# Cross-attention on one core: operand addresses, the first table load, a query copy and the bias load

## The chip, the core and the metric

The kernel runs on one core of a Trainium2 chip. The core has a matrix engine (TensorE, PE in the profile, with its weight loads shown apart as PEld), VectorE (DVE), ScalarE (ACT), GpSimd (POOL) and SyncE (SP). Each has its own instruction queue and works through it in order; they wait for each other through semaphores. DMA transfers are issued from the queues of SP, ACT or POOL. The metric is the device time of one execution in microseconds; lower is better. Operands lie in SBUF, 128 partitions wide; where this text gives the address of a tile, it is the byte offset inside a partition, and it is the allocator's, the same in every execution.

## The reference

Thirty-two batches of queries attend to 77 context rows each. Three of the four attention branches of the reference get an empty slice of the context (it has just the 77 text rows), so they add nothing, and what is left is

```python
# x: (32, 512, 640)   ctx: (32, 77, 1024)   20 heads of 32
q = heads(x @ to_q_w)
k, v = heads(ctx @ to_k_w), heads(ctx @ to_v_w)
p = softmax(q @ k.T / sqrt(32))
out = merge(p @ v) @ to_out_w + to_out_b + x
```

All of it is float32.

## The kernel before

A float32 product is made of three passes over halves: every large operand is split into a high part and a remainder (`split`, L88: a ScalarE copy that rounds, then a VectorE or GpSimd subtraction), and PE adds high·high, high·low and low·high into one PSUM bank (`PAIRS`, L117). Those matmuls have 128x128 weights and 512 streamed columns. Scores and the product with the values are left in plain float32; the trace shows two PE records for each of those.

The order of work is written by hand; no scheduler changes it. It has four stretches.

*Context* (0 to 251 us). Keys and values of all 2464 context rows are computed in five groups (four of 512 rows and one of 416). `load_context` (L139) and `load_weights` (L92) issue the loads; `first` (L271) takes the first group chunk by chunk while the weights still arrive: for chunk k it splits the context (`ct`), the key weights (`wk_s`) and the value weights (`wv_s`), does 15 key matmuls (`pk`) and 9 value matmuls (`pv`). Ahead of it 16 matmuls on a tile of zeros (L269) keep PE busy. In later groups 120 key and 120 value matmuls stand in a row. Results go through DRAM (`k_dram`, `v_dram`). Queues: SP issues most loads, ACT issues two quarters of the first key-weight chunk, POOL issues the first value weights after a small instruction that waits for the first context piece (`pause`, L297).

*Slots* (264 us to the end). There are 160 slots, n = 5b + j for batch b and head group j of four heads (`slot`, L649). Slot n does on PE the scores of n (`sc`, L458, weights `qt`, moving `kb`), the first nine matmuls of an output projection of an earlier batch (`po`, L571, weights `wo_s`, moving `at`), the 15 matmuls of the queries of n+1 (`pq`, L436, weights `wq_s`, moving `xt` or `xu`), the last six of `po`, and in every second slot the values of two earlier slots (`pa`, L518, weights `vb`, moving `raw`). The other engines do the row maxima (`nm`, DVE), the exponentials (ACT, L480), the division by the row sums (`pn`, POOL, L492), the transpose of the probabilities (`z`, DVE, L499), the move of `z` into `raw` (`move_p`, SP, L504), the copy of the queries out of PSUM (`qt`, `copy_q`, L444), splits of `x`, and bias and residual (POOL).

*The fill* is slots 0 to 8, while the pipeline has not got its full distance. There `copy_q` is on VectorE, and `transpose_p(n - 1)` stands ahead of it in a slot, apart from slots that `copied` names (L654: 3 and 4), in which copy comes first and transpose and `move_p` follow. In slot 6 `load_bias` (L411) issues five DMAs on SP: `bias` (one row broadcast to 128 partitions) and four quarters of `bias_y`. The semaphores of SP's DMAs go round in a ring of eight, so an issue waits until the DMA eight issues earlier has landed. The first reader of `bias_y` is `bias_of` (L550) in slot 9; `bias` is read in the last stretch.

*The end* (`end`, L746) finishes the last batch.

Addresses of the matmul operands modulo 512 bytes, before. Slices that a matmul takes of `wk_s`, `wv_s`, `wq_s`, `wo_s`, `ct`, `xt`, `xu`, `at` and `raw` start at multiples of 512 bytes inside their tiles, so each row holds for all matmuls of its kind:

| matmuls | weights | moving |
|---|---|---|
| `pk` | `wk_s` 352 | `ct` 480 |
| `pv` | `wv_s` 480 | `ct` 480 |
| `pq` (most) | `wq_s` 128 | `xt` 128 |
| `pq` (45 of 2400, slots 4 to 8) | `wq_s` 128 | `xu` 64 |
| `po` | `wo_s` 64 | `at` 64 |
| `sc` | `qt` 192 | `kb0` 128 + 308 j, `kb1` 160 + 308 j |
| `pa` | `vb` 192 + 128 i | `raw` 64 |

Of the kernel before, what the change touches and what calls it, by code (L numbers as in the profile page):

```python
# [8 lines left out]
F32 = mybir.dt.float32  # L9
FPR = mybir.dt.float32r  # L10
AF = mybir.ActivationFunctionType
ALU = mybir.AluOpType
# [11 lines left out]
P = 128  # L24
Q = 32
# [3 lines left out]
HPC = 4  # L29
# [8 lines left out]
def kernel(  # L38
# [25 lines left out]
    nc = tc.nc  # L64
    B, S, C = x.shape
    CA = ehs.shape[2]
    NT = B * NKEY
    NQ = S // P
    NC_ = C // P
    NK = CA // P  # L70
    HALF = C // 2
    G = 512
# [19 lines left out]
    def load_weights(w, k0, kn, permuted=True, queues=(nc.sync,) * 4, tag="wraw"):  # L92


        raw = kvw.tile([P, 2, C], F32, tag=tag, name="wraw", bufs=3 if tag == "wraw" else 2)
        if permuted:
            rows = w.rearrange("(q c i) n -> q i c n", q=4, i=Q)
            for q, queue in enumerate(queues):
                queue.dma_start(raw[q * Q : (q + 1) * Q, :kn], rows[q, :, k0 : k0 + kn])
        else:  # L100
            rows = w.rearrange("(c p) n -> p c n", p=P)
            nc.sync.dma_start(raw[:, :kn], rows[:, k0 : k0 + kn])
        for k in range(kn):
            wraws[id(w), k0 + k] = raw[:, k]

    def split_weights(dst, w, k, scale=None, turned=False):

        part = wraws.pop((id(w), k))
        if scale is not None:
            nc.scalar.mul(part, part, scale)  # L110
        hi, lo = dst[:, 0, :], dst[:, 1, :]
        if turned:
            part = part.rearrange("p (q c i) -> p c q i", q=4, i=Q)
            hi, lo = (d.rearrange("p (c q i) -> p c q i", q=4, i=Q) for d in (hi, lo))
        split(hi, lo, part)
# [23 lines left out]
    def load_context(g, *counts):  # L139

        g0, gn = GROUPS_KV[g]
        src = ehs_flat[g0 : g0 + gn, :].rearrange("(a j) (q u) -> q j a u", j=Q, q=4)
        if g not in css:
            css[g] = kvc.tile([P, G // Q, NK * Q], F32, tag="cs", name="cs"), [0]
        cs, done = css[g]
        for kn in counts:
            cols = slice(done[0] * Q, (done[0] + kn) * Q)
            for q in range(4):
                nc.sync.dma_start(  # L149
                    cs[q * Q : (q + 1) * Q, : gn // Q, cols], src[q, :, :, cols]  # L150
                )
            done[0] += kn
# [37 lines left out]
    def keys(g, j, k, *passes):  # L190
        w = wk_s[:, :, :, j * P : (j + 1) * P]
        context_product(pks, "pk", g, j, k, w, psk, *passes)
# [69 lines left out]
    ctx.enter_context(tc.manual_schedule(engines=ENGINES))  # L262


    zero = kvt.tile([P, G], FPR, name="zero")
    nc.vector.memset(zero.bitcast(F32), 0.0)
    warm = psk.tile([P, G], F32, tag="ps", name="warm")
    for _ in range(16):
        nc.tensor.matmul(warm, zero[:, :P], zero, start=True, stop=True)  # L269

    def first(*ks):  # L271

        for k in ks:
            transpose_context(0, k)
        for k in ks:
            if k == 0:
                split_weights(wk_s[:, k], wk, k)
            split_context(0, k)
            if k == 0:
                for n in (0, 2, 1):  # L280
                    for j in range(NC_):
                        keys(0, j, k, (n,))
            else:
                split_weights(wk_s[:, k], wk, k)
                for j in range(NC_):
                    keys(0, j, k)
            part = wraws.pop((id(wv), k))
            for (c0, c1), dst in zip(WV, wv_s):
                split(dst[:, k, 0], dst[:, k, 1], part[:, c0:c1])
            for j in range(3):  # L290
                values_of_chunk(0, j, k, psk)

    load_context(0, 1)
    load_weights(wk, 0, 1, queues=(nc.scalar, nc.scalar, nc.sync, nc.sync))
    pause = kvt.tile([Q, Q], F32, name="pause", bufs=1)
    probe = css[0][0][:Q, 0, :Q]
    nc.gpsimd.tensor_tensor(pause, probe, probe, ALU.add)  # L297
    load_weights(wv, 0, 1, queues=(nc.gpsimd,) * 4, tag="ws")
    load_context(0, 1)
    load_weights(wk, 1, 1)  # L300
# [95 lines left out]
    raws, ats, sms, pqs, pas, xrs, pos, scs, nms = ({} for _ in range(9))  # L396


    kbs = [main.tile([P, NC_, NKEY], F32, name=f"kb{n}") for n in range(2)]
    vbs = [main.tile([KPAD, NC_, HPC, HD], F32, name=f"vb{n}") for n in range(2)]  # L400
    pnb = []
# [9 lines left out]
    def load_bias():  # L411
        biases.append(late[0].tile([P, C], F32, name="bias"))
        biases.append(late[0].tile([P, U], F32, name="bias_y"))
        nc.sync.dma_start(biases[0], bo.unsqueeze(0).to_broadcast([P, C]))
        for q in range(4):
            nc.sync.dma_start(
                biases[1][q * Q : (q + 1) * Q, :],
                bo[q * U : (q + 1) * U].unsqueeze(0).to_broadcast([Q, U]),
            )
# [229 lines left out]
    def slot(n, beside=()):  # L649
# [1 line left out]
        ahead, more = n + 1 < N, b + 1 < B  # L651
        og, oc = b - GROUP[j][0], GROUP[j][1]
        filling = n < NC_ + 2
        copied = n in (3, 4)  # L654
        xsplits = (SPLIT_X if b else {0: (2,), 1: (3,), 2: (4,)}).get(j, ()) if more else ()
        turns = TRANSPOSE_X.get(j, ()) if more and b > 1 else ()
        taken = takes.get(n, ())
# [74 lines left out]
                low_a(m)  # L732
        if n in EARLY_X:
            split_x(2, EARLY_X[n])
        if n == NC_ + 1:
            load_bias()
        for c in xsplits if n != PAIRED - 1 else ():
            split_x(b + 1, c)
# [120 lines left out]
```

## Time and profile before

| | us |
|---|---|
| timed runs | 1737.1, 1742.2, 1742.19 (median 1742.19) |
| profiled execution, its own time | 1736.4 |
| span of its trace, first to last instruction | 1734.4 |
| PE busy | 1724.8 (99%) |
| ACT busy | 1129.3 |
| POOL busy | 985.5 |
| DVE busy | 975.0 |

The granted TensorE clock is 1.000 over the span. Busy time of PE is modelled at the ends of matmuls, which are pipelined; how fast it really goes is read from the distance between starts, or from the chain of work that ended last, in which a piece of PE runs from the end of one matmul to the end of the next. A line of that chain gives start, duration, what, and how many instructions were merged.

### The profile page before, as it was taken

To read this page: it belongs to the slowest core of one execution; us is meant where nothing else is said; L and a number is where in the kernel's file an instruction comes from. 1 tells how busy PE (TensorE), PEld (TensorE's weight loads), DVE (VectorE), ACT (ScalarE), POOL (GpSimd) and SP (SyncE) were. 2 spreads that over 40 slices of the span, in tenths; PEclk is the share of its full clock that TensorE was granted. 3 is DMA by queue.
4 is the path that set the end of the run, shared out by engine and by line. 5 is a ranking of instruction groups with operands and counts; after the bars stand their busy time and mean duration, and the time that the engine had idled before them with its cause. 6 is when DMAs were issued, how large, how long until landed. Compare 5 with 4: busy or idle time off the path is not lost.

```text
span 1734.4 us, 36819 instructions
## 1 busy us (share of the span) xinstructions
PE 1724.8 (99%) x12461; PEld 1312.0 (76%) x12461; DVE 975.0 (56%) x1559; ACT 1129.3 (65%) x5697; POOL 985.5 (57%) x658
## 2 busy tenths in 40 slices
PE   9999999999999999999999999999999999999999
PEld 7888898677777777777777777777777777777777
DVE  5342225756666566665665656556666566665653
ACT  3131126877777777777777777777777777777771
POOL 1000026666666666666666666666666666666665
PEclk9999999999999999999999999999999999999999
DMA  9846566978888888898988888888979798888875
GB/s 186 161 85 177 124 123 145 230 158 195 177 194 174 190 175 191 187 193 176 196 186 179 192 179 184 178 187 183 194 175 200 162 203 173 190 178 190 174 169 158
DMA packets 363979, 306.50 MB, mean 177 GB/s; under 512 B 88784, under 2 KB 292176, under 8 KB 363792
## 3 DMA queue, kind: packets, MB, share of 16 engines
q1 hardware_dynamic: 361200, 297.02, 79.3%
q0 software_dynamic: 2496, 6.97, 1.4%
q8 instruction: 99, 1.62, 0.4%
q14 instruction: 88, 0.72, 0.1%
q10 hardware_dynamic: 96, 0.16, 0.0%
HBM read 120.36 MB, written 57.88 MB: 103 GB/s over the span
## 4 chain that ended last, share of the span: by engine, by line
PE 98%; DMA 1%; SPq 0%; DVE 0%; issue 0%; ACT 0%; POOL 0%; DVEq 0%; ACTq 0%; POOLq 0%
PE po L571 32%; PE pq L436 31%; PE sc L458 10%; PE pa L518 8%; PE pk L182 8%; PE pv L182 8%; PE po L603 1%; DMA raw<-z 0%; DMA bias<-in_L_xattn_to_out_b_dram 0%; SPq L508 0%; DMA wraw<-in_L_xattn_to_k_w_dram 0%; POOL pn L492 0%; SPq L149 0%; DVE z L499 0%; DVE qt L445 0%
## 5 line engine op out<-in xcount | busy, mean ns | idle before, releaser
L480 ACT ACTIVATE pn<-sc,nm 128x77 f32<-128x77 f32 x2560 | 789.2, 364 | 228.8 <-DVE nm L470 191.8
L492 POOL TENSOR_TENSOR pn<-pn,rs 128x1232 f32<-128x1232 f32 x160 | 363.7, 2273 | 483.1 <-DVE rs L490 479.3
L480 ACT ACTIVATION_READ_ACCUMULATOR pn<-sc,nm 128x1 f32 x2560 | 623.3, 244 | 0.0
L571 PE MATMUL po<-at,wo_s 128*128 128x512 f32 x2325 | 601.0, 399 | 0.0
L436 PE MATMUL pq<-xt,wq_s 128*128 128x512 f32 x2355 | 564.9, 391 | 0.0
L436 PEld LDWEIGHTS pq<-xt,wq_s 128*128 128x128 f32 x2355 | 441.5, 188 | 97.2
L571 PEld LDWEIGHTS po<-at,wo_s 128*128 128x128 f32 x2325 | 424.5, 188 | 99.4 <-issue 0.8
L470 DVE TENSOR_REDUCE nm<-sc 128x4 f32<-128x308 f32 x640 | 261.4, 471 | 69.4 <-PE sc L458 69.3
L499 DVE STREAM_TRANSPOSE z<-pn 128x1536 f32<-128x1536 f32 x160 | 283.0, 1769 | 1.0 <-POOL pn L492 0.9
L458 PEld LDWEIGHTS sc<-kb,qt 32*128 32x128 f32 x5120 | 157.3, 186 | 97.6 <-ACT at L532 62.9
L259 POOL TENSOR_TENSOR xt<-xs,xt 128x512 fp32r<-128x512 f32 x157 | 198.1, 1287 | 36.0 <-ACT xt L258 36.0
L581 DVE STREAM_TRANSPOSE ot<-po 128x512 f32<-128x512 f32 x155 | 111.1, 717 | 189.2 <-PE po L571 189.2
L585 POOL TENSOR_TENSOR xs<-xs,ot 128x512 f32<-128x512 f32 x155 | 200.1, 1291 | 2.4 <-DVE ot L581 2.3
L552 POOL TENSOR_TENSOR xs<-xs,bias_y 128x640 f32<-128x640 f32 x124 | 193.5, 1572 | 7.3
L458 PE MATMUL sc<-kb,qt 32*128 32x77 f32 x5120 | 180.9, 277 | 1.9 <-DVE qt L445 1.8
L532 ACT CAST at<-pa 128x512 fp32r<-128x512 f32 x160 | 94.4, 590 | 134.7 <-PE pa L518 134.7
L490 DVE RECIPROCAL rs<-sm 128x16 f32<-128x16 f32 x160 | 40.4, 253 | 223.2 <-ACT pn L480 223.1
L518 PE MATMUL pa<-raw,vb 96*32 96x512 f32 x1280 | 154.9, 599 | 1.4 <-DMA raw<-z 1.4
L537 DVE TENSOR_TENSOR at<-pa,at 128x512 fp32r<-128x512 f32 x160 | 109.8, 686 | 79.1 <-ACT at L532 79.1
L182 PE MATMUL pk<-ct,wk_s 128*128 128x512 f32 (+1 forms) x600 | 136.1, 386 | 1.3 <-ACT ct L89 1.3
L182 PE MATMUL pv<-ct,wv_s 128*128 128x512 f32 (+1 forms) x600 | 134.1, 382 | 0.0
L182 PEld LDWEIGHTS pk<-ct,wk_s 128*128 128x128 f32 x600 | 112.8, 188 | 22.8 <-ACT ct L89 1.7
(41 smaller groups left out, 693.6 us busy)
## 6 DMA issues: line engine op xcount, KB each, us to landing
raw<-z SPq DMA_DIRECT2D x640, 192.0 KB, 4.4
xs<-in_x_dram SPq DMA_DIRECT2D x256, 320.0 KB, 6.4
out_dram<-xs SPq DMA_DIRECT2D x127, 320.0 KB, 5.1
vb<-v_dram SPq DMA_DIRECT2D x32, 240.0 KB, 5.6
kb<-k_dram SPq DMA_DIRECT2D x32, 192.5 KB, 6.2
cs<-in_ctx_dram SPq DMA_DIRECT2D x12, 512.0 KB, 9.1
k_dram<-ks POOLq DMA_DIRECT2D x20, 256.0 KB, 2.4
v_dram<-vs SPq DMA_DIRECT2D x80, 64.0 KB, 2.2
```

Source lines behind the costliest of these rows:

```text
L182: nc.tensor.matmul(held[j][:, :gn], w[:, k, a, :], cts[g, k][:, c, :gn], start=(k == 0 and n == 0), stop=(k == NK - 1 and n == 2),)
L259: low.tensor_tensor(parts[1], src, parts[0].bitcast(F32), ALU.subtract)
L436: nc.tensor.matmul(pqs[n], wq_s[:, k, a, j * P : (j + 1) * P], xts[b, k][:, c, :], start=(k == 0 and m == 0), stop=(k == NC_ - 1 and m == 2),)
L458: nc.tensor.matmul(sc[:, t, :NKEY], qt[r, t * P : (t + 1) * P], kbs[b % 2][r, j, :], start=True, stop=True, tile_position=(i * HD, 0),)
L470: nc.vector.tensor_reduce(nms[n][:, i], sc[:, :, :NKEY], AX.X, ALU.max, negate=True)
L480: nc.scalar.activation(pnb[n % 2][:, at, :NKEY], sc[:, t, :NKEY], AF.Exp, bias=nms[n][:, i, t : t + 1], accum_out=sms[n][:, at : at + 1],)
L492: nc.gpsimd.tensor_tensor(pf, pf, rs.unsqueeze(2).to_broadcast([P, NQ * HPC, NKEY]), ALU.mult)
L499: nc.vector.transpose(z.rearrange("p c h t j -> p (h t) c j"), pn.rearrange("p a (c i) -> p a c i", i=Q),)
L518: nc.tensor.matmul(pas[n][i * HD : (i + 1) * HD, :].rearrange("p (a q) -> p a q", q=P), vb[:, i, :], raw[:, :, i, :], start=True, stop=Tru ...
L552: nc.gpsimd.tensor_tensor(part, part, biases[1].unsqueeze(1).to_broadcast([P, 4, U]), ALU.add)
L571: nc.tensor.matmul(pos[b, c], wos[0][:, k, a, c * P : (c + 1) * P], ats[b * NC_ + k][:, d, :], start=(k == 0 and m == 0), stop=(k == NC_ - ...
L585: nc.gpsimd.tensor_tensor(part, part, ots.pop((b, c)).rearrange("p (a i) -> p a i", i=Q), ALU.add)
```

## The change

Five edits go together.

1. Addresses. `zero` gets one buffer instead of two; `pause` grows from 128 to 512 bytes; a tile `early` of 512 bytes is new; a tile `align` of 64 bytes, which nothing uses, is put at the front of the pool `main`. So `wk_s` moves to 480 modulo 512 (with `ct` and `wv_s` where they were), and everything in `main` and behind it moves up by 64 bytes: `xu`, `at`, `wo_s` and `raw` to 128, `qt` to 256, `kb0` to 192 + 308 j, `kb1` to 224 + 308 j, `vb` to 256 + 128 i. `wq_s`, `xt`, `ct` and `wv_s` stay. `pk` then has 480 and 480, and all `pq` and `po` have 128 and 128; for `sc` and `pa` the distance between the two operands stays as it was.
2. ScalarE copies 32 columns of `zero` into `early` ahead of its two DMA issues, and its first table load stands ahead of that copy. Before, the table load stood behind the two issues and the wait for the key weights.
3. In `first`, the context is split ahead of the key weights in every chunk (in chunk 0 it was the other way round), and the passes of chunk 0 go 0, 1, 2 and not 0, 2, 1. There are 15 matmuls on zeros and not 16.
4. Slot 5 is added to the slots in which `copy_q` stands ahead of `transpose_p` and `move_p`.
5. `load_bias` moves from slot 6 on SP's queue to slot 3 on GpSimd's.

```diff
--- before.py
+++ after.py
@@ -262,10 +262,10 @@
     ctx.enter_context(tc.manual_schedule(engines=ENGINES))
 
 
-    zero = kvt.tile([P, G], FPR, name="zero")
+    zero = kvt.tile([P, G], FPR, name="zero", bufs=1)
     nc.vector.memset(zero.bitcast(F32), 0.0)
     warm = psk.tile([P, G], F32, tag="ps", name="warm")
-    for _ in range(16):
+    for _ in range(15):
         nc.tensor.matmul(warm, zero[:, :P], zero, start=True, stop=True)
 
     def first(*ks):
@@ -273,28 +273,24 @@
         for k in ks:
             transpose_context(0, k)
         for k in ks:
-            if k == 0:
-                split_weights(wk_s[:, k], wk, k)
             split_context(0, k)
-            if k == 0:
-                for n in (0, 2, 1):
-                    for j in range(NC_):
-                        keys(0, j, k, (n,))
-            else:
-                split_weights(wk_s[:, k], wk, k)
+            split_weights(wk_s[:, k], wk, k)
+            for passes in ((0,), (1,), (2,)) if k == 0 else ((0, 1, 2),):
                 for j in range(NC_):
-                    keys(0, j, k)
+                    keys(0, j, k, passes)
             part = wraws.pop((id(wv), k))
             for (c0, c1), dst in zip(WV, wv_s):
                 split(dst[:, k, 0], dst[:, k, 1], part[:, c0:c1])
             for j in range(3):
                 values_of_chunk(0, j, k, psk)
 
+    early = kvt.tile([P, P], F32, name="early", bufs=1)
     load_context(0, 1)
+    nc.scalar.copy(early[:, :Q], zero[:, :Q].bitcast(F32))
     load_weights(wk, 0, 1, queues=(nc.scalar, nc.scalar, nc.sync, nc.sync))
-    pause = kvt.tile([Q, Q], F32, name="pause", bufs=1)
+    pause = kvt.tile([P, P], F32, name="pause", bufs=1)
     probe = css[0][0][:Q, 0, :Q]
-    nc.gpsimd.tensor_tensor(pause, probe, probe, ALU.add)
+    nc.gpsimd.tensor_tensor(pause[:Q, :Q], probe, probe, ALU.add)
     load_weights(wv, 0, 1, queues=(nc.gpsimd,) * 4, tag="ws")
     load_context(0, 1)
     load_weights(wk, 1, 1)
@@ -396,6 +392,7 @@
     raws, ats, sms, pqs, pas, xrs, pos, scs, nms = ({} for _ in range(9))
 
 
+    main.tile([P, HPC * NQ], F32, name="align")
     kbs = [main.tile([P, NC_, NKEY], F32, name=f"kb{n}") for n in range(2)]
     vbs = [main.tile([KPAD, NC_, HPC, HD], F32, name=f"vb{n}") for n in range(2)]
     pnb = []
@@ -411,9 +408,9 @@
     def load_bias():
         biases.append(late[0].tile([P, C], F32, name="bias"))
         biases.append(late[0].tile([P, U], F32, name="bias_y"))
-        nc.sync.dma_start(biases[0], bo.unsqueeze(0).to_broadcast([P, C]))
+        nc.gpsimd.dma_start(biases[0], bo.unsqueeze(0).to_broadcast([P, C]))
         for q in range(4):
-            nc.sync.dma_start(
+            nc.gpsimd.dma_start(
                 biases[1][q * Q : (q + 1) * Q, :],
                 bo[q * U : (q + 1) * U].unsqueeze(0).to_broadcast([Q, U]),
             )
@@ -651,7 +648,7 @@
         ahead, more = n + 1 < N, b + 1 < B
         og, oc = b - GROUP[j][0], GROUP[j][1]
         filling = n < NC_ + 2
-        copied = n in (3, 4)
+        copied = n in (3, 4, 5)
         xsplits = (SPLIT_X if b else {0: (2,), 1: (3,), 2: (4,)}).get(j, ()) if more else ()
         turns = TRANSPOSE_X.get(j, ()) if more and b > 1 else ()
         taken = takes.get(n, ())
@@ -732,7 +729,7 @@
                 low_a(m)
         if n in EARLY_X:
             split_x(2, EARLY_X[n])
-        if n == NC_ + 1:
+        if n == 3:
             load_bias()
         for c in xsplits if n != PAIRED - 1 else ():
             split_x(b + 1, c)
```

## The prediction, on record before the result

> **What bounds the kernel now.** I read the page first (busy time and chain), then the chain in order of time, then the records of single tiles, then the timeline of the start and of the fill.
>
> ```profile
> span 1734.4 us, 36819 instructions
> PE 1724.8 (99%) x12461; PEld 1312.0 (76%) x12461; DVE 975.0 (56%) x1559; ACT 1129.3 (65%) x5697; POOL 985.5 (57%) x658
> ...
> PE po L571 32%; PE pq L436 31%; PE sc L458 10%; PE pa L518 8%; PE pk L182 8%; PE pv L182 8%; PE po L603 1%; DMA raw<-z 0%; DMA bias<-in_L_xattn_to_out_b_dram 0%; SPq L508 0%; DMA wraw<-in_L_xattn_to_k_w_dram 0%; POOL pn L492 0%; SPq L149 0%; DVE z L499 0%; DVE qt L445 0%
> ```
>
> PE is the bound from end to end, and the set of matmuls doesn't change (but for one on zeros). So time can come from two places only: the few microseconds in which PE waits (start, fill), and the rate at which its matmuls follow each other. The rate isn't the same everywhere. The chain in order of time, context stretch:
>
> ```profile
> 64.24 27.89 PE pk L182 x120
> 92.12 27.21 PE pv L182 x120
> ...
> 174.42 27.89 PE pk L182 x120
> ...
> 229.52 22.42 PE pk L182 x120
> ...
> 255.35 9.04 PE pv L182 x48
> ```
>
> Same shapes, same moving tiles, one behind the other: 120 key matmuls take 27.89, that is 232.4 ns each, 120 value matmuls 27.21, or 226.8. What differs is the place of the weights: 352 against 480 modulo 512, with the moving operand at 480. In the last group, with 416 columns, keys take 187 ns and values 188: no difference there. The records of the two moving tiles of the queries say the same:
>
> ```profile
> L436 PE MATMUL pq<-xt,wq_s x2355: 387/389/506, 251.8 to 1690.4; 128*128 128x512 f32 x197
> ...
> L436 PE MATMUL pq<-xu,wq_s x45: 390/394/398, 301.0 to 329.2; 128*128 128x512 f32 x45
> ```
>
> With both at 128 the median is 389 ns, with `xu` at 64 it is 394. Equal is faster, by about 5 ns a matmul. In the slots all operands of `po` and nearly all of `pq` are already equal within a matmul, but the two kinds stand at different places (64 and 128). Two slots of the chain, and then the 15 `pq` matmuls of the second slot cut into the first ten and the last five:
>
> ```profile
> 905.33 2.30 PE po L571 x9
> 907.62 3.41 PE pq L436 x15
> 911.04 1.37 PE po L571 x6
> ...
> 915.33 2.24 PE po L571 x9
> 917.56 3.44 PE pq L436 x15
> ```
> ```profile
> 917.56 2.31 PE pq L436 x10
> ```
> ```profile
> 919.87 1.13 PE pq L436 x5
> ```
> ```profile
> 917.18 3.40 PEld L436 LDWEIGHTS pq<-xt,wq_s 128*128 128x128 f32 x15
> ```
>
> Behind the switch from `po`, ten matmuls take 231 ns each and then five take 226, the rate of the value matmuls. The first weights of `pq` are loaded from 917.18, while the last `po` matmul is still in the chain (to 917.56): one pair with operands at 64 and 128. I read this as a phase between the weight load and the stream that such a pair disturbs and that takes up to ten matmuls to come back.
>
> **The change, part by part**, against the profiled execution (1736.4, of which the span is 1734.4; two timed runs are at 1742.2, one at 1737.1, so it lies at the lower of two levels 5 us apart).
>
> *Addresses, keys.* Groups 1 to 3 have 120 key matmuls each of 512 columns: 3 x (27.89 - 27.21) = -2.0. Nothing hides it or takes it away, as the chain runs on PE from 64 to 252 us. Group 4 gains nothing. Group 0 is in the start, below. Ends: 0 and -2.7, the latter if group 4 gained in proportion.
>
> *Addresses, slots.* After the change `po` and `pq` all stand at 128, so a settled phase should live through both switches. 15 matmuls at 226.8 ns are 3.40. Slots come in two kinds that alternate: 3.44 becomes 3.40 (-0.04) and 3.41 becomes 3.40 (-0.01). The six `po` after `pq` take 1.37, at 226.8 they would take 1.36: -0.01 in both. That is -0.07 a pair; slots 8 to 159 are 76 pairs: **-5.3**. The nine `po` behind the scores also start unsettled (2.30 and 2.24; nine at the settled rate are 2.04), but there `wo_s`, `qt`, `kb`, `vb` and `raw` all move by the same 64 bytes, so I leave that cost. Better end: the 2.30 also becomes 2.24, -0.13 a pair, -9.9. Worse end: the phase never settles, and all of it runs at the 231 ns of those ten; that is the third rival, +12.9.
>
> *Addresses, `xu`.* 45 x 5 ns = -0.2, in the fill, where other waits take it up: 0.
>
> *The start.* Chain and timelines of the first microseconds:
>
> ```profile
> 3.31 2.76 DMA wraw<-in_L_xattn_to_k_w_dram
> ...
> 6.16 1.28 ACT L89
> ...
> 7.45 0.72 ACT wk_s L89
> 8.18 0.53 ACT ct L89
> ...
> 8.75 3.77 PE pk L182 x15
> ...
> 20.16 3.49 PE pk L182 x15
> ```
> ```profile
> 0.74 0.93 ACTq L99 DMA_DIRECT2D wraw<-in_L_xattn_to_k_w_dram  x2
> ```
> ```profile
> 4.88 0.71 DVE L157 STREAM_TRANSPOSE craw<-cs 128x512 f32<-128x512 f32 x1 [3.47 <-DMA cs<-in_ctx_dram]
> ...
> 19.28 0.83 DVE L90 TENSOR_TENSOR wk_s<-wraw,wk_s 128x640 fp32r<-128x640 f32 x1 [1.39 <-ACT wk_s L89]
> ```
> ```profile
> 1.46 6.00 PE L269 MATMUL warm<-zero 128*128 128x512 f32 x16 [1.46 <-DVE zero L266]
> ```
> ```profile
> DMA  0079879999999999999999999999999999999920
> ```
>
> The key weights land at 6.07; then table load 1.28, weight copy 0.72 and context copy 0.53 stand in a row, and PE begins at 8.75. After: the table load runs from 0.74 to 2.0 under the transfers, `early` takes some 0.2 by its 32 columns, and the two ACT issues follow to 3.15, ahead of SP's last one at 3.31, whose landing ended the wait and should still end it. The context (ready at 4.88 + 0.71 = 5.59) is copied while the weights land, weights 6.1 to 6.9; PE, with one matmul on zeros (6.00/16 = 0.38) less, is free at 7.1. So the first key matmul comes 1.6 earlier. That doesn't last: the DMA engines are busy from 2 to 34 us (last row, 40 slices of 0 to 35 us), and the remainder of chunk 2's weights is ready at 19.28 + 0.83 = 20.11, where its first user, the third matmul of `pk`, starts at 20.16 + 2 x 0.23 = 20.6. Only 0.5 can be kept; against it stand two quarters issued 1.5 later to a full DMA queue. I take -0.4. Better end -0.9 (all loads land a bit earlier), worse +0.4 (the 160 KB delayed are 0.8 us of the DMA, and half of it is not made up). The new order of copies and passes is hidden by the same loads. From chunk 5 on the loads are ahead and keys run at the new rate, 15 x 5.6 ns x 3 chunks = -0.3.
>
> *The fill.* Waits, chain, and timelines of VectorE and GpSimd:
>
> ```profile
> PE pa L518 <- DMA raw<-z: 1.4, 2, 0.9
> ```
> ```profile
> 310.78 1.13 PE sc L458 x32
> ...
> 319.52 7.87 DMA bias<-in_L_xattn_to_out_b_dram
> ...
> 328.67 4.07 DMA raw<-z
> ...
> 332.87 1.07 PE pa L518 x8
> ```
> ```profile
> 308.28 1.78 DVE L499 STREAM_TRANSPOSE z<-pn 128x1536 f32<-128x1536 f32 x1 [0.38 <-POOL pn L492]
> 309.99 0.65 DVE L445 COPY qt<-pq 128x512 f32<-128x512 f32 x1
> 311.48 0.25 DVE L490 RECIPROCAL rs<-sm 128x16 f32<-128x16 f32 x1 [0.84 <-ACT pn L480]
> ```
> ```profile
> 300.23 2.28 POOL L492 TENSOR_TENSOR pn<-pn,rs 128x1232 f32<-128x1232 f32 x1 [2.32 <-DVE rs L490]
> 305.97 2.28 POOL L492 TENSOR_TENSOR pn<-pn,rs 128x1232 f32<-128x1232 f32 x1 [3.46 <-DVE rs L490]
> ```
> ```profile
> L204 POOL DMA_DIRECT2D k_dram<-ks x20 | 10.9, 544 | 188.9 <-ACT ks L202 188.3 <-issue 0.2
> ```
>
> Bias: its first DMA takes 7.87 to land, SP's ring makes the issue of slot 7's `raw` wait for it (chain, 319.52 to 328.67), and PE stands 0.9 for that `raw`. Without the five issues on SP that `raw` lands some 3 us before its use: -0.85, and next in line is nothing that the chain shows. On GpSimd five issues at 544 ns are 2.7, in the gap of 3.46 between two divisions (302.5 to 305.97): hidden by 0.7; without that cover the division, the transpose behind it and the scores come later by what is over, +1 at the most by an issue at 0.9 each.
>
> The copy: in slot 5 it moves ahead of a transpose of 1.78 and can start as the queries end (about 309.0), so the scores of slot 6 come some 0.8 earlier. But slot 7's copy hangs on the division of slot 5, whose reciprocal (311.48) waits for ACT's exponentials, and those don't move. So most comes back as a wait of slot 7; the maxima of slot 6, now behind the transpose, win 0.25, and that I take. Together **-1.1**; ends -1.9 and +0.5.
>
> Sum: -2.0 - 5.3 - 0.4 - 0.3 - 1.1 = -9.1; 1736.4 - 9.1 = 1727.3 for an execution like the profiled one. On the two levels of the timed runs it is 1728.0 and 1733.1. The median of the new runs may be on either; I give the middle, 1731.
>
> [...]
>
> **The rivals.**
> First, keys gain and the switches don't: what settles in ten matmuls is the change of PSUM bank or of tile and not the 64 bytes. For it: both come at the same switch. Against it: `pv` changes its bank every 24 matmuls inside 27.21 and keeps 226.8 in the mean. 1736.4 - 2.0 - 0.4 - 0.3 - 1.1 = 1732.6 (1738.4 on the upper level), a gain of 0.2%.
> Second, addresses do nothing: keys are slow because of something else in their stretch. Then -0.4 and -1.1 remain: 1734.9, or 1740.7. Against it: `xu` shows the same 5 ns in another stretch.
> Third, slower: the phase of the slots rests on where `po` stands to the scores, and with all at 128 it doesn't settle. Place: every `po` and `pq` in slots 8 to 159. Price: `pq` at 231 ns, 2 x 15 x 0.231 = 6.93 against 6.85; the six `po` 1.39 against 1.37, twice; the nine `po` 2.30 against 2.24 in every second slot: +0.17 to a pair, x 76 = +12.9. With the rest 1736.4 + 12.9 - 3.8 = 1745.5, or 1751.3. It decides from about +0.12 a pair on, where the time passes 0.3% above before. For it: the start behind the scores is 2.30 in one kind of slot and 2.24 in the other with the same addresses modulo 512, so modulo 512 isn't the whole of it. Against it: `pq` at 128 and 128 does settle.
>
> **How the numbers follow.** My forecast has 0.66, the first rival 0.14, the second 0.07, the third 0.09; 0.04 is for more than forecast (the better end of the slots, 1722.7). The time is that of the forecast. 0.3% is about what a measurement here can tell from no change, 5.2 us: below 1737.0 is faster, above 1747.4 slower. The forecast gains 9.1 with bounds that leave it within 0.3% one time in ten, the first two rivals are within it, the third is above. Faster 0.64, same 0.27, slower 0.09. The range 1723 to 1739 runs from the better end of the forecast to the first rival on the upper level, and leaves out the third and part of the second.
>
> **What would show it.** In the chain after: `pk` x120 at 27.2; `pq` x15 at 3.40 in both kinds of slot and `po` x6 at 1.36; the `xu` median at 389; PE's first `pk` at about 7.1 but chunk 2's only some 0.4 earlier; no bias in the chain and no wait for `raw` in slot 8; a wait of PE ahead of slot 7's scores in place of slot 6's; five GpSimd issues between two divisions without shifting the second. Wrong it would be if `pq` still shows 3.44, or if the nine `po` take more than 2.30.

## The result, and the profile after

The changed kernel takes 1731.56 us (median of six executions, 1730.28 to 1735.23). The kernel before took 1741.14 (six executions with the three of its own page among them, 1737.1 to 1743.99). The ratio is 0.9958, with a 95% interval of 0.9945 to 0.9972. (Ratios here and below are taken over the executions that can be compared and are not the quotients of the two medians.) So it is faster by 0.28 to 0.55%, and the median lies half a microsecond from the forecast. Its terms came out less evenly, and one has the wrong sign.

The profiled execution took 1730.84. The first lines of its page, then its chain in order of time (start, length, engine, what), from the context stretch to slot 9:

```profile
span 1728.6 us, 36822 instructions
...
PE 1720.0 (100%) x12460; PEld 1313.9 (76%) x12460; DVE 974.6 (56%) x1559; ACT 1129.0 (65%) x5698; POOL 987.1 (57%) x663
```

```profile
63.49 27.20 PE pk L182 x120
90.69 27.20 PE pv L182 x120
...
226.69 22.40 PE pk L182 x120
249.09 3.43 PE pq L433 x15
...
335.07 2.29 PE po L568 x9
```

The key matmuls now take what the value matmuls take: 27.20 for 120, where they took 27.89. Two slots from the steady part of the same chain:

```profile
913.09 2.24 PE po L568 x9
915.33 3.40 PE pq L433 x15
918.73 1.36 PE po L568 x6
...
921.15 2.29 PE po L568 x9
923.44 3.41 PE pq L433 x15
926.85 1.36 PE po L568 x6
```

In the kind of slot whose nine `po` take 2.24, `pq` went from 3.44 to 3.40. In the other kind it stays at 3.41, and the six `po` are at 1.36 in both. The two moving tiles of the queries, by tile:

```profile
L433 PE MATMUL pq<-xt,wq_s x2355: 388/389/794, 248.9 to 1685.0; 128*128 128x512 f32 x197
...
L433 PE MATMUL pq<-xu,wq_s x45: 388/389/628, 298.1 to 329.7; 128*128 128x512 f32 x45
```

`xu` now has the median of `xt`, 389 where it had 394. The maxima, 794 and 628 ns where they were 506 and 398, belong to what went wrong.

The two spans differ by 5.8 us, and the chains say where. One more row of the kernel before, the nine `po` of slot 9:

```profile
335.00 2.27 PE po L571 x9
```

| stretch | before | after | difference | forecast |
|---|---|---|---|---|
| to the first key matmul of group 1 | 64.24 | 63.49 | -0.75 | -0.7 |
| groups 1 to 3, to the start of group 4 | 165.28 | 163.20 | -2.08 | -2.0 |
| group 4, to the first `pq` | 22.42 | 22.40 | -0.02 | 0 |
| fill, to the nine `po` of slot 9 | 83.06 | 85.98 | **+2.92** | **-1.1** |
| from there to the end | 1399.4 | 1393.5 | -5.9 | -5.3 |

Each start is read from a chain row and subtracted from the next one. Everything but the fill came out within 0.6. The fill lost 2.9 where a gain of 1.1 was expected. By stretches of 12 us, the fill of the kernel before and then of the kernel after (columns: stretch, its length, the busy time of PE, weight load, VectorE, ScalarE, GpSimd, then granted clock, DMA share and GB/s):

```profile
299.00:311.00 12.00, 11.24 (x110) 7.46 (x103) 10.11 (x17) 11.65 (x71) 5.82 (x3) 1.00 0.75 193
311.00:323.00 12.00, 11.66 (x119) 7.85 (x118) 9.68 (x16) 11.27 (x68) 5.81 (x3) 1.00 1.09 257
323.00:335.00 12.00, 11.15 (x111) 7.67 (x107) 5.82 (x10) 9.49 (x44) 7.39 (x5) 1.00 0.89 198
```

```profile
299.00:311.00 12.00, 12.00 (x114) 8.29 (x113) 9.61 (x17) 11.77 (x71) 8.70 (x9) 1.00 0.99 257
311.00:323.00 12.00, 10.27 (x66) 6.74 (x65) 7.20 (x11) 9.28 (x56) 3.74 (x3) 0.72 1.13 210
323.00:335.00 12.00, 11.45 (x114) 7.87 (x110) 5.76 (x11) 8.91 (x39) 6.67 (x4) 1.00 0.82 167
```

In the first stretch PE no longer waits, a gain of 0.76. In the second PE waits 1.73 instead of 0.34, and the granted clock is 0.72 on average: by an estimate from these two figures, 10.27 us of matmuls at 0.72 do the work of 7.4, a loss of 2.9. The third gains 0.3. That is -0.76 + 1.39 + 2.9 - 0.3 = +3.2, against 2.92 in the chain. The DMA columns can't be compared row by row: the stretches are fixed in time, and the work of the kernel after stands 2.85 earlier in them. Taken 2.85 later, at the same work, the kernel before has DMA shares of 0.94, 1.09 and 0.88 at 261, 234 and 200 GB/s. So the DMA engines were nearly as busy there before, and the bias came on top. In slices of 3 us the clock goes down to half:

```profile
314.00:317.00 3.00, 2.54 (x34) 2.33 (x35) 1.09 (x4) 1.26 (x4) 2.30 (x2) 0.56 1.11 217
317.00:320.00 3.00, 3.00 (x9) 2.32 (x8) 1.69 (x4) 2.97 (x20) 1.19 (x1) 0.50 1.20 165
320.00:323.00 3.00, 3.00 (x16) 1.69 (x14) 2.38 (x3) 2.05 (x14) 0.00 (x0) 0.80 1.10 201
```

PE's timeline of the fill shows the waits (in brackets: idle time before the group, and what ended it); it is the wait for `qt` of slot 7's scores, behind one for `raw`, after which the clock falls:

```profile
311.98 1.06 PE L515 MATMUL pa<-raw,vb 96*32 96x512 f32 x8 [0.30 <-DMA raw<-z]
314.46 2.00 PE L455 MATMUL sc<-kb,qt 32*128 32x77 f32 x32 [1.42 <-DVE qt L442]
332.95 1.06 PE L515 MATMUL pa<-raw,vb 96*32 96x512 f32 x8 [0.55 <-DMA raw<-z]
```

VectorE's timeline shows why that `qt` is late:

```profile
311.96 1.78 DVE L496 STREAM_TRANSPOSE z<-pn 128x1536 f32<-128x1536 f32 x1 [1.06 <-DMA raw<-z]
313.67 0.65 DVE L442 COPY qt<-pq 128x512 f32<-128x512 f32 x1
```

In this slot the copy stands behind the transposition, and that waits 1.06 for a `raw` transfer to be done with `z`. Most of the 1.42 is not the work of `raw`, though: with the same order of copies and the bias in slot 6 (the kernel with edit 4 alone, below) the wait is 1.12, and the transposition is released by the division. The late `raw` adds 0.30 to it, and the 0.30 of the wait ahead.

These rows count PE's time; they don't yet say what set the end of the fill. The chain, which follows back what released what, runs from 308.47 to the last `pa` of the timeline, at 332.95, over three transfers of `raw`, each issued as the one ahead of it lands:

```profile
308.47 8.26 DMA raw<-z
...
316.75 9.81 DMA raw<-z
...
326.57 6.24 DMA raw<-z
```

The first of them was issued 6 us before the clock fell. So in this execution a part of what the slow clock cost lies beside these transfers: had the transfers taken the same time, PE at full clock would have come earlier to that `pa` and waited longer there. How much of the 2.92 would be left at full clock this trace can't say; the kernel with all but the addresses, below, shows it.

And the DMA issues from 296 to 336 us (KB each, median us from issue to landing), before and then after:

```profile
raw<-z SPq DMA_DIRECT2D x24, 192.0 KB, 4.6
```

```profile
raw<-z SPq DMA_DIRECT2D x24, 192.0 KB, 7.1
```

`raw`, which PE needs in every slot, takes 7.1 to land instead of 4.6. GpSimd's timeline shows that the issues themselves cost nothing:

```profile
299.54 0.62 POOL L411 DMA_DIRECT2D bias<-in_L_xattn_to_out_b_dram  x1
300.15 2.01 POOL L413 DMA_DIRECT2D bias_y<-in_L_xattn_to_out_b_dram  x4
303.06 2.28 POOL L489 TENSOR_TENSOR pn<-pn,rs 128x1232 f32<-128x1232 f32 x1 [0.90 <-DVE rs L487]
```

They end at 302.16, and the next division still waits 0.90 for its own input.

The start, by the timelines of ScalarE, VectorE and PE:

```profile
0.74 1.28 ACT L289 ACT_TABLE_LOAD   x1 [0.74 <-PEq L840]
1.45 0.86 ACTq L99 DMA_DIRECT2D wraw<-in_L_xattn_to_k_w_dram  x2
```

```profile
5.92 0.71 DVE L157 STREAM_TRANSPOSE craw<-cs 128x512 f32<-128x512 f32 x1 [4.51 <-DMA cs<-in_ctx_dram]
```

```profile
7.96 3.69 PE L182 MATMUL pk<-ct,wk_s 128*128 128x512 f32 x15 [0.16 <-ACT wk_s L89]
```

The first key matmul comes at 7.96, 0.8 earlier than before and not 1.6 as forecast, because the context landed 1.0 later (transposed from 5.92, before from 4.88).

### The profile page after: what moved, and what is told of

Same layout as the page of the kernel before. It is cut to its first block, busy times and chain, and to the rows that moved or that the text cites. A ratio compares the mean times of both kernels' runs of the same rounds, so it can differ in the third digit from the quotient of the medians.

```text
span 1728.6 us, 36822 instructions
## 1 busy us (share of the span) xinstructions
PE 1720.0 (100%) x12460; PEld 1313.9 (76%) x12460; DVE 974.6 (56%) x1559; ACT 1129.0 (65%) x5698; POOL 987.1 (57%) x663
## 3 DMA queue, kind: packets, MB, share of 16 engines
q8 instruction: 99, 1.62, 0.4%
## 4 chain that ended last, share of the span: by engine, by line
PE 96%; DMA 2%; DVE 1%; SPq 1%; issue 0%; ACT 0%; POOL 0%; DVEq 0%; POOLq 0%; ACTq 0%
PE po L568 32%; PE pq L433 31%; PE sc L455 10%; PE pa L515 8%; PE pv L182 7%; PE pk L182 7%; DMA raw<-z 1%; PE po L600 1%; DMA wraw<-in_L_xattn_to_k_w_dram 1%; SPq L99 0%; DVE z L496 0%; DMA cs<-in_ctx_dram 0%; SPq L149 0%; DVE wk_s L90 0%; ACT wk_s L89 0%
```

## The experiments

Two theories were at odds over each half of the change. For the addresses: equal places modulo 512 save the time (forecast), against a kernel whose gain comes from the start or the fill alone. For the fill, once the loss was seen: a bias load moved into a full stretch of the DMA engines costs it, against the order of copies in slot 5, and against GpSimd's queue as such. "Before" is each time the kernel before, timed beside the variant on the same chip.

### The addresses alone, and everything but the addresses

The first kernel is the one before with edit 1 and nothing else (start, slot 5 and bias as they were):

```diff
-    zero = kvt.tile([P, G], FPR, name="zero")
+    zero = kvt.tile([P, G], FPR, name="zero", bufs=1)
...
-    pause = kvt.tile([Q, Q], F32, name="pause", bufs=1)
+    early = kvt.tile([P, P], F32, name="early", bufs=1)
+    pause = kvt.tile([P, P], F32, name="pause", bufs=1)
...
+    main.tile([P, HPC * NQ], F32, name="align")
```

> Only the addresses of the change (zero, early, pause, align as tiles; no other edit). Theory A (operand addresses set PE's rate, and the fill is bound by DMA, so that what comes earlier before the fill is lost in it): 120 key matmuls 27.2 us, queries x15 3.40 or 3.41 in both kinds of slot, the last six po 1.36; from slot 9 to the end 5.9 us shorter than before, the start of slot 9's po as before (335, within 1): 6 us faster than before. Theory B (the gain ahead of the fill is lost only through the fill edits): slot 9's po some 2 us earlier than before, 8 us faster. Rival (addresses do nothing, the rest of the change made the gain): 0.

The second is the changed kernel with the old addresses (`early` takes the place of the second buffer of `zero`):

```diff
-    early = kvt.tile([P, P], F32, name="early", bufs=1)
+    early = kvt.tile([P, G], F32, name="early", bufs=1)
...
-    pause = kvt.tile([P, P], F32, name="pause", bufs=1)
+    pause = kvt.tile([Q, Q], F32, name="pause", bufs=1)
...
-    main.tile([P, HPC * NQ], F32, name="align")
```

> The change without its addresses: all matmul operands at the places of before (early made larger, pause as before, no align), with the table load first, the order in the first chunks, the third copy ahead and the bias on GpSimd's queue. Theory A and B: key matmuls 27.9 per 120, queries 3.44 and 3.41; from slot 9 on as before. The start gains about 0.5 by the loads. If the fill edits cost what the trace after shows (2.9 us), 1 to 3 us slower than before; if they are only swallowed by the DMA, 0 to 0.5 faster. Rival (addresses do nothing): 9 us faster.

The addresses alone: 1730.93 against 1738.23, ratio 0.9950 (0.9933 to 0.9967). Everything but the addresses: 1740.49, ratio 1.0007 (0.9997 to 1.0018), no gain that can be seen. The chains, addresses alone and then all but the addresses:

```profile
64.03 27.20 PE pk L182 x120
...
917.76 3.40 PE pq L438 x15
```

```profile
64.19 27.89 PE pk L182 x120
...
922.34 3.44 PE pq L432 x15
```

The 27.89 and the 3.44 go with the addresses and come back without them. So the gain of the changed kernel is theirs, and the other edits together, without them, give none. Two expectations didn't come out. Without the addresses the first key matmul of group 1 comes at 64.19, against 64.24 before: the edits of the start gained 0.05 and not 0.5. And the interval, 0.5 faster to 3.1 slower than before, doesn't choose between the two fills that were expected. Its trace does, and it answers the question of the result: the fill is the changed one, the clock stays at 1.00 up to slot 9's scores, and its chain runs over three `raw` transfers much like those above (8.28, 10.50 and 5.74). Its waits add up to 5.18 (0.74, 1.42, 1.41 and 1.61) against 1.85, and the nine `po` of slot 9 start at 338.67, 86.78 behind the first `pq` (251.89): 3.7 more than before, 3.3 of it in waits. So transfers as late as these cost the fill some 3 us at full clock too. For the addresses alone the traced execution went as theory A has it: its nine `po` of slot 9 start at 335.26, where they start at 335.00 before, because PE waits 2.65 for a `raw` that SP issues only after the bias (8.91 to land) is there. It is an execution in which the clock fell (mean 0.998). The median, 7.3 us below before, lies between the two theories.

### One address: the 64 bytes in `main` alone

```diff
+    main.tile([P, HPC * NQ], F32, name="align")
```

put into the kernel before and nothing else; `wk_s` stays at 352 modulo 512.

> Before with the 64 bytes of align alone: key weights at 352 as before, po and xu at 128. If the two address gains are separate and add: 120 key matmuls 27.9 as before, queries x15 3.40 and 3.41, the six po 1.36, slot 9 to the end 5.6 shorter, so 5 to 6 us faster than before. If the switch cost came from tiles or banks and not from the 64 bytes: 0.

1732.11 against 1741.26, ratio 0.9952 (0.9935 to 0.9969). Its chain:

```profile
64.41 27.89 PE pk L182 x120
...
908.70 3.41 PE pq L437 x15
...
918.62 3.40 PE pq L437 x15
```

Keys at the old 27.89, slots at the new 3.40. The two address gains are separate: each comes with its own tile, and neither needs the other.

### Another distance: 128 bytes and not 64

```diff
-    main.tile([P, HPC * NQ], F32, name="align")
+    main.tile([P, 2 * HPC * NQ], F32, name="align")
```

With it `po` has its operands at 192, `pq` from `xt` at 128, and `xu` is again at 64 from its weights, on the other side.

> After with the align tile of 128 bytes in place of 64: po at 192 and 192, pq still at 128 and 128, xu at 192 against wq_s at 128; all distances inside scores and values as before. If the distance of 64 at the switch is what unsettles PE: queries x15 again about 3.44 and 3.41 (or up to 3.47), the six po 1.37, 5 to 6 us slower than after, context stretch as after. If it was the absolute place of po (64 being bad, 128 and beyond good): as after. If the sign of the distance matters: queries x15 between 3.40 and 3.44.

1734.8 against 1738.23, ratio 0.9976 (0.9965 to 0.9987): part of the gain is lost.

```profile
906.90 1.39 PE po L568 x6
...
921.58 3.41 PE pq L433 x15
```

Equal within each kind of matmul isn't enough. The six `po` behind `pq` take 1.39, more than with equal places (1.36) and more than in the kernel before, where `po` stood 64 to the other side (1.37); `pq` takes 3.41. So it isn't the size of the distance across a switch alone: its sign counts, or the place itself (192 and not 64), which this one kernel doesn't separate. `xu`, at 192 with its weights at 128, has 394 again.

### The fill: the changed kernel again, and without its edits

The changed kernel once more, with no edit, beside its variants:

> The changed kernel once more, as the yardstick of this call. Six earlier executions: 1730.3 to 1735.2, all with a mean clock of 0.998 or 0.999. The same again, some 8 us below the kernel before.

1731.16 against 1739.07, ratio 0.9948 (0.9931 to 0.9966). In this execution no fall of the clock comes ahead of slot 9: PE waits 1.13, 0.70 and 1.40 in the fill, the nine `po` of slot 9 start at 333.49, and it is they that take 3.72 and not 2.29, as the clock falls behind the 1.40 (0.69 from 332 to 335 us, 0.74 from 335 to 338). From the first `pq` (249.49) that is 84.00, 0.9 more than before, where the execution in the result had 85.98. The kernel with 128 bytes has the same edits 2 to 5 and was traced at a clock of 1.000; there the fill is 331.99 - 248.79 = 83.20, and its chain goes over three `raw` transfers too (6.01, 8.66 and 6.76). So a fill with edits 4 and 5 costs between 0.1 and 3.7 by the execution and its transfers, before what a fall behind it adds. Without edits 4 and 5:

```diff
-        copied = n in (3, 4, 5)
+        copied = n in (3, 4)
...
-        if n == 3:
+        if n == NC_ + 1:
             load_bias()
```

with the bias on SP's queue as before.

> The change without its two fill edits (copy ahead in slots 3 and 4 only, bias back in slot 6 on SP). Theory A (fill bound by DMA whatever comes earlier): slot 9's po starts at about 335 as before and after, time as after, within 1 us. Theory B (one of the fill edits starves PE so long that its clock drops): no half clock between 311 and 323, slot 9's po at about 332, some 3 us faster than after, 12 faster than before.

1728.42 against 1738.23, ratio 0.9938 (0.9923 to 0.9952). By the timeline below its nine `po` of slot 9 start at 330.64 + 1.07 + 1.06 = 332.77, 2.3 ahead of the changed kernel's 335.07 and 0.7 ahead of its 333.49. Then each edit of the fill alone. The bias back on SP's queue in slot 6, the copy of slot 5 kept ahead:

```diff
-        nc.gpsimd.dma_start(biases[0], bo.unsqueeze(0).to_broadcast([P, C]))
+        nc.sync.dma_start(biases[0], bo.unsqueeze(0).to_broadcast([P, C]))
...
-        if n == 3:
+        if n == NC_ + 1:
             load_bias()
```

> After, but the bias back in slot 6 on SP; the third copy ahead stays. If the copy ahead makes the long wait of PE in the fill: PE waits over 1 us ahead of the scores of slot 7, half clock behind it, time as after. If the bias on GpSimd's queue did it: the fill as in the kernel without fill edits, about 3 us faster than after.

1727.74 against 1739.07, ratio 0.9929 (0.9911 to 0.9948). And the copy put back, the bias left in slot 3 on GpSimd:

```diff
-        copied = n in (3, 4, 5)
+        copied = n in (3, 4)
```

> After, but the copy ahead only in slots 3 and 4; the bias stays in slot 3 on GpSimd. If the copy ahead did it: a wait of 0.9 ahead of slot 6's scores and no half clock, 2 to 3 us faster than after. If the bias did it (0.4 MB moved to where the DMA has just filled up): the landing of raw late in slots 6 and 7, time as after.

1731.72, ratio 0.9948 (0.9929 to 0.9968). The loss stays with the bias and goes with it: the changed kernel, timed beside these two, took 1731.16, 3.4 more than with the bias back in slot 6. PE's timelines, without edits 4 and 5 and then with edit 4 alone:

```profile
308.26 1.13 PE L455 MATMUL sc<-kb,qt 32*128 32x77 f32 x32 [0.88 <-DVE qt L442]
320.21 1.13 PE L455 MATMUL sc<-kb,qt 32*128 32x77 f32 x32 [0.29 <-DVE qt L442]
330.64 1.07 PE L515 MATMUL pa<-raw,vb 96*32 96x512 f32 x8 [1.24 <-DMA raw<-z]
```

```profile
313.73 1.13 PE L455 MATMUL sc<-kb,qt 32*128 32x77 f32 x32 [1.12 <-DVE qt L442]
```

The copy ahead takes away the wait of 0.88 at slot 6 and the 0.29 at slot 8 and puts 1.12 in slot 7. In time the two kernels can't be told apart (1728.42 and 1727.74, not timed side by side).

### The queue or the place in time

Two kernels with the one without the other: the bias in slot 3 but on SP's queue, and the bias on GpSimd's queue but in slot 6.

```diff
-        nc.gpsimd.dma_start(biases[0], bo.unsqueeze(0).to_broadcast([P, C]))
+        nc.sync.dma_start(biases[0], bo.unsqueeze(0).to_broadcast([P, C]))
...
```

> After, the bias in slot 3 but on SP's queue. If the place in time (0.4 MB where the DMA engines have just filled up) is what costs: landing of raw 7 us in the median from 296 to 336, half clock in most executions, time as after (1731). If it is GpSimd's queue: raw lands in 4 to 5 us, clock 1.0, about 1728.

```diff
-        if n == 3:
+        if n == NC_ + 1:
             load_bias()
```

> After, the bias on GpSimd's queue but in slot 6 as before. If GpSimd's queue is what costs, beside the eight transfers that SP may have in flight: late raw from slot 7 on, half clock, about 1731. If the place in time costs: about 1728, and without the wait for the bias in SP's ring up to 1 less.

Slot 3 on SP: 1731.51 against 1741.26, ratio 0.9950 (0.9934 to 0.9967). Slot 6 on GpSimd: 1728.97, ratio 0.9936 (0.9918 to 0.9955). The DMA issues from 296 to 336 us, slot 3 on SP and then slot 6 on GpSimd:

```profile
raw<-z SPq DMA_DIRECT2D x23, 192.0 KB, 7.0
```

```profile
raw<-z SPq DMA_DIRECT2D x24, 192.0 KB, 4.2
```

`raw` lands in 7.0 with the bias in slot 3 on SP's queue, 7.1 on GpSimd's; with the bias in slot 6 in 4.2 on GpSimd's and, by the kernel with edit 4 alone, 3.9 on SP's. By these four landings the time at which the transfer starts decides, not its queue. Over all profiled executions the median is 6.1 to 7.3 in the six with the bias in slot 3, and 3.8 to 4.6 in the eight with it in slot 6.

All executions of these kernels with a known clock can be counted by what the clock did. With the bias in slot 3 (the changed kernel twice, all but the addresses, 128 bytes, copy put back, slot 3 on SP) the mean clock is below 1.000 in 46 of 48. With the bias in slot 6 and the new addresses (all or some of them) it is so in 11 of 42, and in the kernel before in 25 of 45. The mean is that of the whole execution; where the clock fell is seen in the profiled ones alone, and there it was in slots 7 to 9, but for some last microseconds of the span (0.88 from 1724 us on in the changed kernel). An execution below 1.000 is mostly some 2 to 8 us longer than one of the same kernel at 1.000 (longer waits ahead of the fall may be a part of that; and of the last kernel below one at 0.999 took 1727.88 and four at 1.000 took 1726.91 to 1728.35): the addresses alone took 1727.8 to 1729.3 in three executions at 1.000 and 1732.5 to 1733.7 in three at 0.998, and the kernel before, beside the kernels of this section, 1736.5 to 1737.1 in three and 1739.3 to 1744.7 in eight.

### More room for the bias

Chunks 3 and 4 of `wo_s`, 640 KB each, are loaded in slots 4 and 5. Here both go in slot 3, and the fill is otherwise that of the kernel before:

```diff
-    WO = {1: (0, 1, 2), 4: (3,), 5: (4,)}
+    WO = {1: (0, 1, 2), 3: (3, 4)}
```

> The change without its fill edits, and the last two of the five output weight loads issued in slot 3 and not in slots 4 and 5, which puts 1.28 MB into the stretch (296 to 299) in which the DMA engines are nearly idle. If the fill's end is set by DMA throughput from 299 to 332: raw of slot 8 lands 2 to 4 us earlier, the wait of 1.2 us for it goes, and no execution falls to half clock: 1 to 2 us faster than without fill edits (about 1727). If the ring of eight holds back the raw issues behind the larger loads: slower.

1726.79 against 1739.07, ratio 0.9920 (0.9901 to 0.9939): the lowest median of the study, though its interval overlaps those of the kernels without edits 4 and 5 and with edit 4 alone. All six executions have a clock of 1.000, within 1.4 us of each other. Its PE waits in the fill are three, and none is for `raw`:

```profile
308.17 1.13 PE L455 MATMUL sc<-kb,qt 32*128 32x77 f32 x32 [0.88 <-DVE qt L442]
314.09 1.13 PE L455 MATMUL sc<-kb,qt 32*128 32x77 f32 x32 [0.17 <-DVE qt L442]
320.13 1.13 PE L455 MATMUL sc<-kb,qt 32*128 32x77 f32 x32 [0.27 <-DVE qt L442]
```

The same with the copy of slot 5 ahead:

```diff
-        copied = n in (3, 4)
+        copied = n in (3, 4, 5)
```

> The change with the bias back on SP in slot 6 (copy ahead kept) and the last two output weight loads in slot 3. If both edits help on their own they add in part: no half clock in any execution, the wait ahead of slot 7's scores about 1, the wait of slot 8 for raw gone, 1726 to 1727 us. If the wait only moves on to the scores of slots 6 and 7: as with the early loads alone (1726.8).

1727.71 against 1741.26, ratio 0.9927 (0.9909 to 0.9945), with waits of 1.13 at slot 7's scores and of 0.82 for `raw`. It is no better; the intervals overlap, and two of its six executions have a clock of 0.999, where none was expected.

## Why the prediction was right, and where it was wrong

*What bounds the kernel.* Right: PE is busy for 1720.0 of 1728.6, and no other engine came into the way of the steady slots.

*Keys.* Right in place and size: -2.08 against -2.0 in the trace, and nothing in group 4. With `wk_s` left where it was, the 27.89 stays.

*Slots.* Right in place: 3.44 became 3.40, 1.37 became 1.36, 3.41 stayed, and the nine `po` behind the scores kept 2.24 and 2.29 or 2.30. The term was -5.3 and the trace gave -5.9; at 76 pairs a hundredth in a row is 0.8 us, so the rows can't say where the 0.6 is from. The reading as a phase that a pair of matmuls with unequal places disturbs agrees with the two experiments on `main`. It is a description; why the place should matter was not tried, nor whether 512 bytes is the period: the distances measured are 64 and 128.

*`xu`.* Right: 394 became 389, and the fill hid it.

*The start.* Close in the sum (-0.75 against -0.7), with luck, and not right in its steps. The first key matmul came at 7.96 and not 7.1, as the context landed later, and ScalarE's DMA issues went out at 1.45, beside the table load (0.74 to 2.02) and not behind it as the sum had them: the description of the core, by which an engine works through its queue in order, doesn't hold for these issues. The gain can't be put down to the edits: the same kernel again starts group 1 at 63.89 (-0.35), the kernel without the addresses at 64.19 (-0.05), the one with the addresses alone at 64.03 (-0.21), and the last kernel of the experiments, with addresses and edits of the start, at 64.36 (+0.12). In time too they don't show: the kernel with the addresses alone, without the edits of the start, took 1727.8 to 1729.3 at full clock, and the one with them and the old fill 1727.6 to 1728.5.

*The fill.* Wrong: the failed step is the bias at -0.85, "hidden by 0.7". Its price was worked out on the queue that it leaves and on the engine that it moves to; that part held, as the five issues fit in their gap. What was left out is the transfer itself, 0.4 MB in slot 3, on DMA engines that the later chunks of `wo_s` and the slots' own `raw` all but fill just then (share 0.94 at the same work before, 0.99 and then 1.13 after). `raw` lands 2.5 later, and what waits for `raw` comes late: the fill ends on a chain of three such transfers (8.26, 9.81 and 6.24), and the sign "no wait for `raw` in slot 8" failed with 0.55. In medians timed side by side the place of the bias is worth 3.4 (1731.16 against 1727.74). PE's time in the profiled fill divides into 0.42 more of waits (2.27 against 1.85) and, for the rest of the 2.92, some 2.5, the granted clock at half, of which the prediction had nothing. But that is where PE's time went, and not what made the fill long: with the same fill edits, transfers as late (8.28, 10.50 and 5.74) and a full clock the kernel with all but the addresses lost 3.7 there, 3.3 of it in waits, and with shorter ones (6.01, 8.66 and 6.76) the kernel with 128 bytes lost 0.1. By this comparison the slow clock mostly filled time in which PE would have waited. Where the clock falls at slot 9, with no transfer to wait for beside it, it does cost: with the addresses alone the scores and the nine `po` there take 1.94 and 4.14 in place of the 1.06 and 2.27 to 2.29 of the other chains, 2.7 more. The copy of slot 5 went as forecast: it moved the wait of slot 6 to slot 7. With the wait it moved also lies the 1.42 after which the clock fell; but with the copy put back and the bias kept the clock falls as well, and without the bias the copy does no harm.

*The total.* The sum without the fill, 1736.4 - 2.0 - 5.3 - 0.7 = 1728.4, is that of the kernel without edits 4 and 5: 1728.42. For an execution like the profiled one the forecast was 1727.3, and the profiled one took 1730.84, 3.5 above it: the fill is 4.0 off, and the slots give 0.6 of it back. The median still lies near 1731 because the forecast put the timed runs of the kernel before on two levels 5 us apart and took the middle. The upper level goes with a mean clock below 1.000 in later executions of that kernel (beside the last kernels 1736.5 to 1737.1 at 1.000 and 1739.3 to 1744.7 below it). None of them was profiled; in the two kernels that have its fill (addresses alone, 64 bytes alone) the traces show the clock fall at slot 9. So most likely a loss by the clock was already in part of before's runs. The agreement of the median with 1731 thus owes something to luck: a level that was averaged in stands for a loss that wasn't seen.

*The rivals.* The first (keys gain, switches don't) fell with the kernel that has the 64 bytes alone, the second (addresses do nothing) with the one that has all addresses alone (27.20 for 120 key matmuls and not 27.89, ratio 0.9950). The third (the phase doesn't settle) didn't come in the changed kernel; something like it shows in small with 128 bytes, where the six `po` behind `pq` got slower.

*What stays open.* Whether a wait brings the clock down, and when. In the fills of the profiled executions no single wait of 1.24 or less was followed by a fall, and each of 1.6 and more was (1.62, 1.61, 1.74, 2.65; 2.64 in the kernel with the 64 bytes alone; at 1.62 another of 1.42 came before the fall). Of five between 1.40 and 1.42 three were followed by one and two weren't, both in the kernel with all but the addresses. The length of one wait isn't the whole of it: at the start PE waits 2.08 with the addresses alone, and the 15 key matmuls behind that wait take 3.70, no more than the 3.77 that they take in the kernel before at a clock of 1.00 (where the DMA share is 1.26 and 1.17 from 6 to 10 us). The same kernel falls in one execution and not in another: with the addresses alone the mean clock is 0.998 in three and 1.000 in three. Why the same transfers take 6.01, 8.66 and 6.76 in one execution and 8.26, 9.81 and 6.24 in another is open too. Nor was it tried what sets the start of the nine `po` behind the scores at 2.24 or 2.29.

## What to carry to other kernels

Where TensorE bounds a kernel, compare equal matmuls at different addresses, and try the same place modulo 512 bytes for the weights and the moving operand, also across the switches between kinds of matmul; here a few tiles of padding are worth 0.5% (0.3 to 0.7% by the interval) without an instruction moved. (It paid with 512 columns; the key matmuls with 416 took the same time at both places, 22.42 and 22.40 for 120.) Before a transfer is moved, look at the DMA share of the stretch in which it will land, and not only at a gap in the queue that issues it; here that share was 0.94, and `raw` landed in 7.1 instead of 4.6. And look at the granted clock of several executions: behind waits of 1.4 to 2.7 us it fell here in eight traced executions, in one of them for 2.7 us more at slot 9, and a median may hold a loss that the profiled execution doesn't show.

## What the runs showed of the hardware that was not expected

- Identical matmuls of 512 columns run at 226.7 ns or at 232.4 ns (27.20 and 27.89 for 120) by the place of their weights to their moving operand modulo 512 (480 and 480, or 352 and 480). Behind a switch between kinds at 64 and 128 ten matmuls took 231 ns each before the next five took 226. Six `po` behind `pq` take 1.36 with no distance between the kinds, 1.37 with `po` 64 below and 1.39 with it 64 above.
- Waits of PE of 1.4 to 2.7 us in slots 7 to 9 were followed by a fall of the granted clock in eight traced executions: in four of them a slice of 3 us stands at 0.50, in the other four the lowest slice has a mean of 0.61 to 0.70. Waits of 1.42 and 1.41 in the kernel with all but the addresses were not followed by one, and behind a wait of 2.08 at the start 15 key matmuls took 3.70. That the wait itself brings the clock down is not shown.
- 0.4 MB moved three slots ahead, into a stretch with a DMA share of 0.94, brought the median landing of 192 KB from 3.8 to 4.6 us (eight profiled executions) to 6.1 to 7.3 (six).
- ScalarE's DMA issues didn't wait for the table load and the copy that stand ahead of them in the program: the load ran from 0.74 to 2.02 and the copy from 2.04, the issues from 1.45 on.
